# A four-layer convolution and attention kernel: another layout for the convolution results kept in device memory, and five images instead of four with a chunk convolved on VectorE

## The chip, the cores and the metric

The kernel runs on one core of one Trainium2 chip. The metric is the device time of one execution in microseconds (us), lower is better. The core has five engines that run side by side: TensorE (PE, matrix products into PSUM), VectorE (DVE), ScalarE (ACT), GpSimd (POOL) and SyncE (SP). SP and ACT also issue transfers (DMAs) between the device memory and the on-chip memory SBUF. Each engine works through its own queue in the order in which the program was laid out, and waits on semaphores where it needs another engine's result.

## The reference

The input x is 8 images of 384 channels and 32 x 32 pixels, in float32. Four residual layers follow each other, each on a group norm of x. Only the first matters here:

```python
def _dwproj(x, dw, g, b, pw):                     # for q, k and v
    y = depthwise_3x3(x, dw)                      # zero padding, one 3x3 filter per channel
    y = gelu(_bn(y, g, b))                        # batch norm over all 8 images and pixels
    return einsum('oc,bchw->bohw', pw, y)
q, k, v = _dwproj(gn(x), ...q), _dwproj(gn(x), ...k), _dwproj(gn(x), ...v)
attn = softmax(einsum('bhcn,bhcm->bhnm', q, k) * scale)      # 8 heads of 48 channels, 1024 pixels
x = x + _bn(w_out @ (attn applied to v), g_out, b_out)
```

The batch norm takes mean and variance over all images. So the three depthwise convolutions of all 8 images must be done, and their raw results kept somewhere, before the first GELU can run. The other three layers (a mixture of four small networks, a convolution with ternary weights, and an attention with sampled positions) are not touched by the change.

## The kernel before, in words

An image is held as 128 partitions x 3 chunks x 1024 pixels: channel 3p + c lies on partition p in chunk c.

**The convolution stage (first 390 us).** Each image b is group-normed by `norm(b)` in three steps. `begin` takes statistics on VectorE. `middle` (`gn_spread`) multiplies them with a small matrix on TensorE, into a PSUM bank of the pool `ps_mm`, and copies the result to `ga_a` (L118). `end` (`gn_scale`, then `affine`) does a second such product and writes the normed image into one of two padded buffers `pads`. Then the convolution runs in groups. A group g = 0 to 8 takes 42 channels (every third partition of chunk g // 3): `stack` copies them three times, shifted by a row, into a tile of 126 partitions (L318, three transfers on SP), and TensorE makes q, k and v of those 42 channels at once as 3 matmuls (one for each horizontal tap) for each half of the pixels, each of which leaves two records in the trace. The row 3 * i + v of the result `y` is channel i of q, k or v (v = 0, 1, 2). ScalarE copies each half from PSUM to `y` (L387), VectorE takes its statistics (L388), and ScalarE issues the stores to device memory (L394). Group `NGC` = 9 takes the two partitions left over in each of the three chunks (18 rows). `ps_mm` has four banks, so two groups' worth.

For the images in `ON_V` (0, 2, 4, 6) the groups 6, 7 and 8, chunk 2, are left out on TensorE. VectorE makes them itself, tap by tap (`convolve`: 9 instructions for each of q, k, v, L290 and L292, then `finish` with two statistics, one store and three small transfers that put the statistics where the groups would have put them). These steps wait in a list `taps`, and two of them are emitted after each group.

The order is written out by hand as a list `work` of (image, group). Before group n, the stacks of the groups up to nine ahead (`AHEAD`) are issued, and `begins` says at which n the norm of an image starts; its three steps follow at n, n + 1 and n + 2. At the end of the last image, `load_b(0)` loads the first image of the next stage, and `bn_moments` combines the statistics of a group over all images. The tile framework lays the program out for each engine: by this order, but an instruction whose inputs are ready in its own estimate may pass one that is not. It also inserts the waits, and transfers share a limited number of completion semaphores, so a transfer on SP can wait for an earlier one on ACT.

**The hand-over (390 to 405 us).** `bn_params` makes scale and shift (its power function runs on GpSimd, L97), L407 to L435 move them by small matmuls to the channel order, and the result is `ss0`. `values_tile` clears two tiles `vt` on GpSimd (L505). The weights of the next stage are loaded on SP (L512, L515), into memory that the convolution stage used.

**The attention stage (405 to about 1480 us).** For each image: `load_b` brings the raw q, k and v tiles in (three tiles of 512 KB for each of three chunks, from the pool `im` with five buffers), ScalarE applies scale, shift and GELU, TensorE projects, and runs the four head pairs of the attention. `gather_last` (into `ql`) and `place_last` (into `att`) are small transfers on SP between the parts. Loads of a coming image are issued when a buffer of `im` comes free.

A branch that is taken only if a softmax sum leaves a range (`redo`) holds the attention in a slower form, and reads `raw` too. It isn't taken in these runs.

Of the kernel before, what the change touches and what calls it, by code (L numbers as in the profile page):

```python
# [7 lines left out]
F32 = mybir.dt.float32  # L8
# [4 lines left out]
B, C, H, W = 8, 384, 32, 32  # L13
N = H * W
P = 128
KC = C // P
# [36 lines left out]
def tile_kernel(ctx: ExitStack, tc: tile.TileContext, i: dict, out: bass.AP):  # L53
    nc = tc.nc
# [148 lines left out]
    def image(name):  # L203
        return im.tile([P, KC, N], F32, tag="im", name=name)

    raw = [dram.tile([B, P, KC, N], F32, name=f"raw{v}") for v in range(3)]
    ss0 = const.tile([P, 3, 2, KC], F32, name="ss0")
    xmv = const.tile([P, B, KC, 2], F32, name="xmv")
    bn0 = bn_tiles(3 * GC, NGC + 1, "qkv")
    ON_V = (0, 2, 4, 6)  # L210
    acts = {}

    def load_b(b):
        acts[b] = {}
        for v in (0, 1, 2) if b == 0 else (2, 1, 0):
            acts[b][v] = image(f"g{v}_{b}")
            load_image(acts[b][v], raw[v][b])

    with ExitStack() as pa:
        wa = pa.enter_context(tc.tile_pool(name="a_w", bufs=1))  # L220
# [54 lines left out]
        def convolve(b, xn):  # L275

            state = {}

            def tap(v, t):
                dy, dx = t // 3 - 1, t % 3 - 1  # L280
                w = cwv[: 3 * GC, v, t : t + 1]
                if t == 4:
                    state["y"] = ya.tile([3 * GC, N], F32, tag="y", name=f"yv{b}_{v}")
                y = state["y"].rearrange("p (h w) -> p h w", h=H)
                r0, r1 = max(0, -dy), H - max(0, dy)
                c0, c1 = max(0, -dx), W - max(0, dx)
                d = y[:, r0:r1, c0:c1]
                f = xn[:, r0 + dy : r1 + dy, c0 + dx : c1 + dx]
                if t == 4:
                    nc.vector.tensor_scalar(d, f, w, None, ALU.mult)  # L290
                else:
                    nc.vector.scalar_tensor_tensor(d, f, w, d, ALU.mult, ALU.add)  # L292

            def finish(v):
                y = state["y"]
                for h in range(2):
                    nc.vector.bn_stats(vst[:, v, h, :], y[:, h * HALF : (h + 1) * HALF])
                nc.scalar.dma_start(out=raw[v][b, : 3 * GC, KC - 1, :], in_=y)
                for t in range(3):
                    nc.sync.dma_start(  # L300
                        out=cst[v : 3 * GC : 3, 3 * (KC - 1) + t, 2 * b : 2 * b + 2, :],
                        in_=vst[t : 3 * GC : 3, v, :, :],
                    )

            steps = []
            for v in range(3):
                steps += [lambda v=v, t=t: tap(v, t) for t in (4, 0, 1, 2, 3, 5, 6, 7, 8)]
                steps.append(lambda v=v: finish(v))
            return steps
# [30 lines left out]
        sts, taps, todo, later, normed = {}, [], {}, list(work), {0}  # L340

        def stacks(n):
            while later and len(work) - len(later) < n and later[0][0] in normed:
# [10 lines left out]
        for n, (b, g) in enumerate(work):  # L354
            if n in begins:
                b2 = begins[n]
                for k, f in enumerate(norm(b2)):
                    todo[n + k] = f, (b2 if k == 2 else 0)
                if b2 + 1 < B and b2 + 1 not in xts:
                    load_x(b2 + 1)  # L360
            if n in todo:
                f, b2 = todo.pop(n)
                f()
                normed.add(b2)
            stacks(n + AHEAD + 1)
            st = sts.pop((b, g))
            nch = GC if g < NGC else GR
# [5 lines left out]
            for h, k in steps:  # L373
# [11 lines left out]
                if k == 2:  # L385
                    hs = slice(h * HALF, (h + 1) * HALF)
                    nc.scalar.copy(y[:, hs], pk[h][: 3 * nch, :])  # L387
                    nc.vector.bn_stats(cst[: 3 * nch, g, 2 * b + h, :], y[:, hs])  # L388
            for v in range(3):
                if g < NGC:  # L390
                    to, of = raw[v][b, g % 3 : 3 * GC : 3, g // 3, :], y[v : 3 * GC : 3, :]
                else:
                    to, of = raw[v][b, 3 * GC :, :, :], y[v * GR : (v + 1) * GR, :]
                nc.scalar.dma_start(out=to, in_=of)  # L394
# [30 lines left out]
        for v in range(3):  # L425
# [66 lines left out]
    with ExitStack() as pb:  # L492
# [9 lines left out]

        def values_tile(s):
            t = wb.tile([P, NT8, 2 * NH0, 32], F32, name=f"vt{s}")
            nc.gpsimd.memset(t, 0.0)  # L505
            nc.gpsimd.memset(t[:, :, :, HQ0 : HQ0 + 1], 1.0)
            vts.append(t)

# [280 lines left out]
    with tc.If(redo > 0):  # L789
        with ExitStack() as pb:  # L790
# [13 lines left out]
            with tc.For_i(0, B) as bi:  # L804
                act = []
                for v in range(3):
                    g = work[v]
                    nc.sync.dma_start(
                        out=g, in_=raw[v][bass.ds(bi, 1)].rearrange("o p c n -> p (o c) n")
                    )  # L810
                    gelu_image(g, v)
                    act.append(g)
                for t in range(NT8):
# [1011 lines left out]
```

## Time and profile before

| What | us |
|---|---|
| median of 3 runs (lowest, highest) | 3829.66 (3827.58, 3834.88) |
| the profiled execution, its own time | 3834.06 |
| the span of that execution in the trace | 3832.2 |
| first convolution matmul, end of the last one | 21.68, 388.2 |
| first projection matmul of the attention stage | 404.93 |
| TensorE busy, of the span | 3646.2 (95%) |
| VectorE busy, of the span | 1823.4 (48%) |
| ScalarE busy, of the span | 1314.7 (34%) |

A line of a group view gives source line, engine, operation, the tile written <- the tiles read, shapes, count | busy us, mean ns of one | idle us just before, and what ended it. A line of a view in order of time begins with start and length in us; merged neighbours carry a count, and a bracket at the end gives the idle time ahead and what ended it. A line of the waits gives total us, number of times, longest. SPq and ACTq are the times that an engine spends issuing transfers.

### The profile page before, as it was taken

The numbers are of one execution on the slowest core, as the hardware profiler recorded it, in microseconds if no ns is written. First come the engines' busy times: TensorE is split into PE (matmuls) and PEld (weight loads), VectorE is DVE, ScalarE is ACT, GpSimd is POOL, SyncE is SP. The second block draws the span as 40 slices with busy tenths as digits, with TensorE's granted clock in tenths as the row PEclk, the third lists the DMA queues.
The fourth block names the chain that finished last, engine by engine and source line by source line (L and its number), as shares of the span: only waits on it lengthen the run. The fifth ranks groups of instructions, "written<-read, shape, count | busy, mean of one in ns | idle before, by whom it ended". The sixth has DMA issues, their size and how long they took to land.

```text
span 3832.2 us, 39353 instructions
## 1 busy us (share of the span) xinstructions
PE 3646.2 (95%) x15754; PEld 1520.9 (40%) x15754; DVE 1823.4 (48%) x2826; ACT 1314.7 (34%) x1557; POOL 235.5 (6%) x170
## 2 busy tenths in 40 slices
PE   7999899999999999999899999999999999999748
PEld 3444333333333333333344445444444444445213
DVE  5876223232323232332256665475656646565544
ACT  2222454554546353534112323223232222313102
POOL 0000000000000000000000100101011010100321
PEclk9999999999999999999899999999999999999868
DMA  6777211121202121111620000101001010010000
GB/s 200 245 235 241 100 53 43 53 61 40 74 24 72 27 69 38 59 49 50 233 81 33 17 33 19 48 17 33 33 17 34 17 50 17 25 42 1 17 17 18
DMA packets 83097, 242.64 MB, mean 63 GB/s; under 512 B 18336, under 2 KB 18864, under 8 KB 82520
## 3 DMA queue, kind: packets, MB, share of 16 engines
q1 hardware_dynamic: 69894, 200.56, 15.7%
q10 hardware_dynamic: 13008, 39.43, 3.0%
q8 instruction: 128, 2.10, 0.2%
q14 instruction: 67, 0.55, 0.0%
HBM read 122.78 MB, written 75.50 MB: 52 GB/s over the span
## 4 chain that ended last, share of the span: by engine, by line
PE 39%; DVE 9%; POOL 1%; issue 1%; ACT 1%; DVEq 0%; ACTq 0%; POOLq 0%
PE y L1251 10%; PE ph L1232 8%; DVE y L1320 5%; PE pq L1367 3%; PE pw L1341 3%; PE s L1504 3%; PE pf L1609 3%; PE pav L1520 2%; PE pss L1546 1%; DVE hd L1218 1%; DVE off L1415 1%; PE pk L1478 1%; PE xsb L1464 1%; PE pv L1487 1%; POOL tap L1323 1%
## 5 line engine op out<-in xcount | busy, mean ns | idle before, releaser
L630 ACT ACTIVATE p<-s 128x1024 f32<-128x1024 f32 x512 | 496.4, 1021 | 497.1 <-PE s L623 496.8
L1251 PE MATMUL y<-hd,w_sb 128*128 128x512 f32 x1080 | 493.4, 601 | 3.6 <-DVE hd L1218 3.6
L638 PE MATMUL pav<-p,vt 64*64 64x512 f32 x4096 | 486.4, 589 | 0.0
L1232 PE MATMUL ph<-h,w_sb 128*128 128x512 f32 x1104 | 483.6, 594 | 0.0
L623 PE MATMUL s<-qk,qk 48*64 48x512 f32 x3072 | 373.1, 600 | 4.4 <-ACT p L630 4.4
L381 PE MATMUL pk<-st,cw_sb 126*126 126x512 f32 x720 | 321.5, 608 | 3.6 <-DVE ga_a L118 3.3
L1232 PEld LDWEIGHTS ph<-h,w_sb 128*128 128x128 f32 x1104 | 207.8, 190 | 252.5 <-issue 249.4
L1251 PEld LDWEIGHTS y<-hd,w_sb 128*128 128x128 f32 x1080 | 198.8, 191 | 250.4 <-issue 236.3
L638 PEld LDWEIGHTS pav<-p,vt 64*64 64x64 f32 x4096 | 156.2, 133 | 285.3 <-issue 285.0
L595 DVE COPY ta<-pav 128x512 f32<-128x512 f32 x64 | 44.3, 692 | 439.1 <-PE pav L638 436.1
L1320 DVE SCALAR_TENSOR_TENSOR y<-h,tap,y 128x961 f32<-128x961 f32 (+1 forms) x184 | 233.5, 1295 | 1.6
L381 PEld LDWEIGHTS pk<-st,cw_sb 126*126 126x126 f32 x720 | 140.1, 197 | 177.7 <-issue 170.7
L1415 DVE SCALAR_TENSOR_TENSOR off<-q,dw_sb,off 128x225 f32<-128x225 f32 (+3 forms) x432 | 209.6, 542 | 1.9
L1240 ACT ACTIVATE hd<-ph,b_sb 128x512 f32<-128x512 f32 x180 | 122.6, 681 | 254.3 <-PE ph L1232 253.9
L623 PEld LDWEIGHTS s<-qk,qk 48*64 48x64 f32 x3072 | 102.6, 133 | 241.6 <-issue 184.7
L1341 PE MATMUL pw<-y,upw 128*128 128x512 f32 x288 | 128.6, 602 | 54.8 <-POOL y L1324 50.1
L78 DVE COPY qk<-pq 128x512 f32<-128x512 f32 x48 | 33.2, 692 | 293.1 <-PE pq L558 281.4
L387 ACT COPY y<-pk 126x512 f32<-126x512 f32 (+1 forms) x136 | 76.2, 583 | 254.4 <-DMA raw<-y 115.9
L1511 ACT ACTIVATE p<-s 128x1024 f32<-128x1024 f32 x96 | 93.0, 1021 | 171.8 <-PE s L1504 171.7
L146 ACT ACTIVATE h<-x,ss_d 128x1024 f32<-128x1024 f32 x42 | 49.6, 1231 | 287.6 <-DVE ss_d L132 287.6
L575 PE MATMUL po<-att,wo_sb 128*128 128x512 f32 x288 | 134.5, 617 | 9.5 <-DMA att<-al 9.5
L1218 DVE TENSOR_TENSOR hd<-hd,cb 128x512 f32<-128x512 f32 x180 | 122.9, 688 | 34.6 <-ACT hd L1240 34.2
(281 smaller groups left out, 4124.0 us busy)
## 6 DMA issues: line engine op xcount, KB each, us to landing
g<-raw SPq DMA_DIRECT2D x72, 512.0 KB
st<-pad SPq DMA_DIRECT2D x180, 168.0 KB
raw<-y ACTq DMA_DIRECT2D x180, 168.0 KB
xa<-in_x_dram SPq DMA_DIRECT2D x24, 512.0 KB
xh<-in_x_dram SPq DMA_DIRECT2D x48, 256.0 KB
f<-in_x_dram SPq DMA_DIRECT2D x24, 512.0 KB
f<-o SPq DMA_DIRECT2D x24, 512.0 KB
o<-ot SPq DMA_DIRECT2D x42, 256.0 KB
```

The costliest lines, as they stand in the source:

```text
L381: nc.tensor.matmul(pk[h].rearrange("p (h w) -> p h w", w=W)[: 3 * nch, :, o0 : o0 + c1 - c0], lhsT=lhs, rhs=rhs, start=(k == 0), stop=(k = ...
L575: nc.tensor.matmul(po, lhsT=wo0[:, c, m * P : (m + 1) * P], rhs=atts[b][:, c, hs], start=(c == 0), stop=(c == KC - 1),)
L623: nc.tensor.matmul(s[64 * k : 64 * k + 64, j * HALF : (j + 1) * HALF], lhsT=kt[r, k0 : k0 + 64], rhs=qt[r, h * HALF : (h + 1) * HALF], sta ...
L630: nc.scalar.activation(p, s, AF.Exp, scale=scale)
L638: nc.tensor.matmul(pav[k][64 * j : 64 * j + 64, :], lhsT=vts[b % 2][r, kc, 2 * hd : 2 * hd + 2, :].rearrange("p a b -> p (a b)"), rhs=p[r, ...
L1218: nc.vector.tensor_tensor(hd, hd, state["cb"], ALU.mult)
L1232: nc.tensor.matmul(ph, lhsT=w1[:, e, c, dc * P : (dc + 1) * P], rhs=state["h1"][c], start=(c == 0), stop=(c == KC - 1),)
L1240: nc.scalar.activation(hd, ph, AF.Relu, bias=b1[:, k : k + 1])
L1251: nc.tensor.matmul(y, lhsT=w2[:, e, dc, m * P : (m + 1) * P], rhs=state[h, k], start=(k == 0), stop=(k == NE * KC - 1),)
L1320: eng.scalar_tensor_tensor(d, f, tap2[:, c, t : t + 1], d, ALU.mult, ALU.add)
L1341: nc.tensor.matmul(pw[:, hs], lhsT=upw2[:, c, m * P : (m + 1) * P], rhs=y[:, c, hs], start=(c == 0), stop=(c == KC - 1),)
L1415: nc.vector.scalar_tensor_tensor(d, f, dw3[:, t : t + 1], d, ALU.mult, ALU.add)
```

## The change

The raw results are now one tensor in the form in which TensorE leaves them: `raw[image, group, 126 rows, pixels]`, and `raw_r` for the remainder group. A group's result is stored with one transfer instead of three. When an image is loaded, `load_raw` picks the rows of q, k or v out of it: three transfers of 42 rows for each chunk and one of two rows, where `load_image` used one of 128 rows. The branch `redo` loads in the same way.

`ON_V` becomes (0, 2, 3, 5, 6). After the groups two and three steps of `taps` are emitted in turn. The stores of the chunk made by VectorE are no longer issued in `finish` but by a new function `keep` four groups later: three strided stores and the three small statistics transfers, all on ScalarE's queue (the small ones were on SP).

The groups of an image come in the order 0, 1, NGC, 2, ... instead of NGC, 0, 1, .... A norm begins four groups earlier than the reach of the stacks instead of two, and its steps are two groups apart. In the last image `load_b(0)` comes at group 1 instead of 5, and the moments of groups 6, 7 and 8 are combined together after group 8. Last, the clearing of the first `vt` tiles on GpSimd is made to wait for the instruction that ends `ss0`.

```diff
-    raw = [dram.tile([B, P, KC, N], F32, name=f"raw{v}") for v in range(3)]
+    raw = dram.tile([B, NGC, 3 * GC, N], F32, name="raw")
+    raw_r = dram.tile([B, 3 * GR, N], F32, name="raw_r")
...
-    ON_V = (0, 2, 4, 6)
+    ON_V = (0, 2, 3, 5, 6)
     acts = {}
+
+    def load_raw(dst, b, v):
+
+        at = slice(b, b + 1) if isinstance(b, int) else b
+        for g in range(NGC):
+            nc.sync.dma_start(
+                out=dst[g % 3 : 3 * GC : 3, g // 3, :],
+                in_=raw[at, g, v : 3 * GC : 3, :].rearrange("o p n -> (o p) n"),
+            )
+            if g % 3 == 2:
+                nc.sync.dma_start(
+                    out=dst[3 * GC :, g // 3, :],
+                    in_=raw_r[at, v * GR + g // 3 : (v + 1) * GR : KC, :].rearrange(
+                        "o p n -> (o p) n"
+                    ),
+                )
...
-            load_image(acts[b][v], raw[v][b])
+            load_raw(acts[b][v], b, v)
...
-                nc.scalar.dma_start(out=raw[v][b, : 3 * GC, KC - 1, :], in_=y)
+                late.append((n_now[0] + 4, lambda: keep(v, y)))
+
+            def keep(v, y):
                 for t in range(3):
-                    nc.sync.dma_start(
+                    nc.scalar.dma_start(
+                        out=raw[b, 3 * (KC - 1) + t, v : 3 * GC : 3, :], in_=y[t : 3 * GC : 3, :]
+                    )
+                    nc.scalar.dma_start(
                         out=cst[v : 3 * GC : 3, 3 * (KC - 1) + t, 2 * b : 2 * b + 2, :],
                         in_=vst[t : 3 * GC : 3, v, :, :],
                     )
...
-        groups = [(NGC, *range(NGC - 3 if b in ON_V else NGC)) for b in range(B)]
+        groups = [[0, 1, NGC, *range(2, NGC - 3 if b in ON_V else NGC)] for b in range(B)]
...
-        begins = {max(2, work.index((b, NGC)) - AHEAD - 2): b for b in range(1, B)}
+        begins = {max(1, work.index((b, groups[b][0])) - AHEAD - 4): b for b in range(1, B)}
...
-                    todo[n + k] = f, (b2 if k == 2 else 0)
+                    todo.append((n + 2 * k, f, b2 if k == 2 else 0))
...
-            for v in range(3):
-                if g < NGC:
-                    to, of = raw[v][b, g % 3 : 3 * GC : 3, g // 3, :], y[v : 3 * GC : 3, :]
-                else:
-                    to, of = raw[v][b, 3 * GC :, :, :], y[v * GR : (v + 1) * GR, :]
-                nc.scalar.dma_start(out=to, in_=of)
-            for _ in range(2):
+            nc.scalar.dma_start(out=raw[b, g] if g < NGC else raw_r[b], in_=y)
+            for _ in range(2 + n % 2):
                 if taps:
                     taps.pop(0)()
+
+            while late and (late[0][0] <= n or n + 1 == len(work)):
+                late.pop(0)[1]()
             if b == B - 1:
-                if g == 5:
+                if g == 1:
                     load_b(0)
-                bn_moments(cst, g, bn0)
+
+                if g < NGC - 3 or g == NGC:
+                    bn_moments(cst, g, bn0)
+                elif g == NGC - 1:
+                    for k in range(NGC - 3, NGC):
+                        bn_moments(cst, k, bn0)
...
-        nc.vector.tensor_tensor(
+        scales = nc.vector.tensor_tensor(
             ss0.rearrange("p v s k -> p v (s k)"), ss0.rearrange("p v s k -> p v (s k)"),
...
-            nc.gpsimd.memset(t, 0.0)
+            zero = nc.gpsimd.memset(t, 0.0)
+
+            tc.add_manual_dep(
+                zero.ins, scales.ins.name, mybir.DependencyInfo(
+                    mybir.DependencyClass.Sync, mybir.DependencyReason.DATA
+                ), reason="scales first",
+            )
```

More of the change, by code (lines that the diff above doesn't have):

```diff
@@ L335, in tile_kernel @@
         AHEAD = 9
-        groups = [(NGC, *range(NGC - 3 if b in ON_V else NGC)) for b in range(B)]
+        groups = [[0, 1, NGC, *range(2, NGC - 3 if b in ON_V else NGC)] for b in range(B)]
         work = [(b, g) for b in range(B) for g in groups[b]]
-        begins = {max(2, work.index((b, NGC)) - AHEAD - 2): b for b in range(1, B)}
-        sts, taps, todo, later, normed = {}, [], {}, list(work), {0}
+        begins = {max(1, work.index((b, groups[b][0])) - AHEAD - 4): b for b in range(1, B)}
+        sts, taps, todo, later, normed, late, n_now = {}, [], [], list(work), {0}, [], [0]
         def stacks(n):
@@ L357, in tile_kernel @@
                 for k, f in enumerate(norm(b2)):
-                    todo[n + k] = f, (b2 if k == 2 else 0)
+                    todo.append((n + 2 * k, f, b2 if k == 2 else 0))
                 if b2 + 1 < B and b2 + 1 not in xts:
                     load_x(b2 + 1)
[L361 to L364, printed above, removed]
+            n_now[0] = n
+            for step in [t for t in todo if t[0] == n]:
+                todo.remove(step)
+                step[1]()
+                normed.add(step[2])
             stacks(n + AHEAD + 1)
@@ L807, in tile_kernel @@
                     g = work[v]
-                    nc.sync.dma_start(
-                        out=g, in_=raw[v][bass.ds(bi, 1)].rearrange("o p c n -> p (o c) n")
-                    )
+                    load_raw(g, bass.ds(bi, 1), v)
                     gelu_image(g, v)
```

## The prediction

> **What bounds the kernel now.** I read the page first (slices), then busy time by stretch, then each engine in order of time over the first 480 us, because the diff touches only the convolution stage, the hand-over, and the loads of the attention stage.
>
> ```profile
> PE   7999899999999999999899999999999999999748
> DVE  5876223232323232332256665475656646565544
> PEclk9999999999999999999899999999999999999868
> ```
>
> A slice is 95.8 us; the convolution stage is the first four. TensorE is nearly full in all of them while VectorE is at 5 to 8 tenths. The stretches (columns: length, then busy of PE, weight load, DVE, ACT, POOL, then granted clock, DMA share, GB/s):
>
> ```profile
> 20.00:390.00 370.00, 358.07 (x844) 151.35 (x844) 258.07 (x379) 100.05 (x156) 6.41 (x7) 0.95 0.70 231
> 390.00:405.00 15.00, 3.32 (x13) 3.07 (x13) 6.36 (x15) 3.23 (x4) 7.59 (x3) 0.59 0.87 321
> 405.00:1480.00 1075.00, 1070.62 (x7036) 397.03 (x7040) 310.52 (x511) 540.76 (x541) 1.82 (x3) 1.00 0.16 50
> ```
>
> So the stage is bound by TensorE (358 of 370 us), VectorE has 112 us free, then comes a hole of some 15 us, then an attention stage in which TensorE is 99.6% busy. TensorE in order of time:
>
> ```profile
> 21.68 8.08 PE L381 MATMUL pk<-st,cwr_sb 18*18 18x512 f32 x12 [9.97 <-DMA st<-pad]
> 29.69 12.69 PE L381 MATMUL pk<-st,cw_sb 126*126 126x512 f32 x24
> ...
> 123.50 2.70 PE L381 MATMUL pk<-st,cwr_sb 18*18 18x512 f32 x12
> 126.13 30.53 PE L381 MATMUL pk<-st,cw_sb 126*126 126x512 f32 x72
> ...
> 287.93 8.23 PE L381 MATMUL pk<-st,cw_sb 126*126 126x512 f32 x12 [3.06 <-DVE ga_a L118]
> ```
>
> A full group of 12 records costs 30.53/6 = 5.09 us, the remainder group (NGC) 2.70. The first two lines are slow: 8.08 instead of 2.70, and 12.69 instead of 10.18. The last line is the kernel's one bad meeting of norm and convolution: the next PSUM bank was held until VectorE copied ga_a, 3.06 us of stall, then 12 records at 8.23 instead of 5.09. VectorE's costs and the waits of the stage:
>
> ```profile
> L388 DVE BATCH_NORM_STATS2 cst<-y 126x6 f32<-126x512 f32 x120 | 79.0, 684 | 64.2 <-ACT y L387 64.1
> L292 DVE SCALAR_TENSOR_TENSOR yv<-xn,cwv_sb,yv 126x992 f32<-126x992 f32 x48 | 59.6, 1241 | 0.6
> L292 DVE SCALAR_TENSOR_TENSOR yv<-xn,cwv_sb,yv 126x961 f32<-126x961 f32 x48 | 58.1, 1211 | 0.9
> ```
> ```profile
> ACT y L387 <- DMA raw<-y: 113.5, 36, 7.8
> DVE cst L388 <- ACT y L387: 71.3, 34, 5.3
> ```
>
> ScalarE spends much of the stage issuing stores, and VectorE waits for its copies. What each transfer costs its queue (ns, min/median/max):
>
> ```profile
> L394 ACTq DMA_DIRECT2D raw<-y x204: 276/774/1872, 30.4 to 393.7; - x102
> L171 SPq DMA_DIRECT2D g<-raw x72: 327/430/902, 361.5 to 1453.1; - x72
> L298 ACTq DMA_DIRECT2D raw<-yv x12: 332/338/1066, 42.5 to 348.7; - x12
> ```
>
> A transfer of every third partition costs 774 ns to issue, an unstrided one 338. And the hand-over and the attention stage's SP queue:
>
> ```profile
> 395.98 3.16 DVE L407 COPY both<-bnsc_qkv 126x10 f32<-126x10 f32 x1
> 399.20 0.17 DVE L408 COPY both<-bnsh_qkv 126x10 f32<-126x10 f32 x1
> ```
> ```profile
> 395.61 3.51 POOL L505 MEMSET vt<- 128x4096 f32 x1
> ```
> ```profile
> 507.13 59.15 SPq L171 DMA_DIRECT2D g<-raw  x5
> 588.44 8.07 SPq L471 DMA_DIRECT2D att<-al  x12
> ```
>
> [...] the same small copy takes 0.17 us, but 3.16 while the memset runs. [...] full groups run at half pace from 29.69 to about 34.5, although narrow matmuls had run since 21.68[...]. [...]
>
> **Part by part.**
>
> *Five images on VectorE instead of four* (3 and 5 in, 4 out). Three full groups go: 3 x 5.09 = **-15.3 us** of TensorE. VectorE gains 27 taps (3 x 0.72 + 12 x 1.241 + 12 x 1.211 = 31.6), 6 statistics (4.1) and one copy (0.7), and loses 6 statistics (4.1): +32 us, about 29 with the overlap of successive instructions. So it goes from 258 to some 288.
>
> *2.5 taps per group.* 150 steps run out at group 60 of 65. Those groups take TensorE 52 x 5.09 + 8 x 2.70 = 286 us at full pace; now the stage takes 1.10 times that (388.2 - 21.7 - 7.9 at the start = 358.6 against 60 x 5.09 + 8 x 2.70 = 327), so 314. VectorE needs some 281 (288 less the last five groups' work). That leaves 33 us, and another 17 can be caught up in the last five groups, where it has no taps. Its waits for other things than ScalarE were 13.2 (images), 9.6 (xn), and 6.3 + 6.2 + 3.0 (norm chain) = 38 us in this stage. So it just fits. I charge **+5 us** for banks held a little longer (bounds -2, when the wider spacing of the norm steps removes the 287.93 stall, and +45, when VectorE is late at many norms).
>
> *Group order 0, 1, NGC, and norms begun 4 ahead, two groups apart.* Groups 0 and 1 read only chunk 0 of the first image. Their three transfers issue from 14.03 (about 0.85 each) and land near 18.5, against 21.68 for the first matmul now: -3. [...] now 8.08 - 2.70 + 12.69 - 10.18 = 7.9 are lost. Together up to -9; I take **-7** (bounds -9 and 0, if the weights are not there or later stacks fall behind).
>
> *One store per group.* ScalarE: 3 x 0.77 becomes 0.34, so some 120 us of issue time go. The convolved chunk's stores become three strided ones and its three small statistics transfers move from SP to ScalarE: 15 x 6 x 0.77 = 69 us, in bursts of 4.6 us, four groups late. A burst delays the next copies by up to 4 us; two groups' worth of PSUM (10 us) hides that, and without it each of 15 bursts would cost its 4 us. Small waits of TensorE for y (7.8 us in all) shrink: **-2** (bounds -6 and +3).
>
> *Hand-over.* The memset waits for the scales, so the locked copy's **-3.0** is certain if its order holds; the two memsets (2 x 3.5 us) then lie in VectorE's 9 us of idleness after the scales. The last copy, at 391.48 behind a store that issued slowly, should come near the last matmul's end: -2.5. Three moments at the end instead of one: +1.1. Image 0's loads, 27 x 0.77 + 9 x 0.4 = 24 us of SP instead of 4, begin eight groups before the end: hidden. But the two loads of image 1 (24 transfers, 17 us) may stand ahead of the weights as six do now (at 380.59, weights at 394.47): +3, bounds 0 and +10. Sum **-1.5**.
>
> *Attention stage.* SP gets 36 transfers per image instead of 9, +20 us of its 177. The last of them start when the values' matmuls free their buffer (566 us in image 0). Twelve take 9 us, and the att transfers stand at 588.44: 22 us of cover. Queued behind are att and ql, for which the output projection (635) and the last pair's scores wait. **+1**, bounds 0 and +15.
>
> Sum: -15.3 + 5 - 7 - 2 - 1.5 + 1 = **-19.8**; I round to -18, as stage sums seldom arrive whole. Against the profiled span 3832.2 that is 3814; the profiled execution (3834.06) lay 4.4 us above the median of 3829.66, so for the median **3812**.
>
> **Rivals.**
> (1) *VectorE is the new bound and eats most of it.* For: 281 + 38 us of 314. Against: taps fill its waits, and a late VectorE no longer waits for ScalarE (71 us now). Gain 4 to 11: 3819 to 3826.
> (2) *Slower: PSUM banks held at the norms.* Each norm puts two small results into the convolution's four banks, freed only by a VectorE copy in its queue. Behind taps of 1.2 us the 287.93 episode repeats; it cost 3.06 + 8.23 - 5.09 = 6.2 us, and happened at one of 14 such places. From about six more places on (37 us against a gain of some 25 without the +5) it is slower by over 0.2%; at eight, 3855. For: VectorE is busy for 281 of 314 us, its waits not counted. Against: the chain's steps are now two groups apart.
> (3) *The saving is absorbed*: the order that is built isn't the one written, SP's loads reach TensorE in each image (3 us x 7), or the weights come 10 us late: within 7.7 us of now.
>
> **How the numbers follow.** A measurement here can tell about 0.2%, 7.7 us. The sum as worked out (gain 12 to 26): 0.52, own range 3804 to 3818. Rival 1: 0.20, of which three quarters are still over 0.2%. Rival 3: 0.08. Rival 2: 0.16, a quarter of that within 0.2%. A gain above 26: 0.04. Faster 0.52 + 0.15 + 0.04 = 0.71; same 0.05 + 0.08 + 0.04 = 0.17; slower 0.12. The range 3800 to 3836 leaves out about 0.16.
>
> **What would show it.** Right: first full group before 20 us and full pace by 24; last convolution matmul near 366; VectorE's wait for y well under 71 us; the L407 copy at 0.17 us; TensorE over 99% in the attention stage. Wrong: more stalls before L381 put down to ga_a or ve_a; the weights issued over 10 us after the last matmul; att or ql landing behind g<-raw; a longer hole.

## The result, and the profile after

The changed kernel takes **3852.52 us** (median of 4 runs, 3849.47 to 3855.56), against 3832.27 for the kernel before on the same chip: a ratio of 1.0054, with a 95% interval of 1.0036 to 1.0071. It is slower by half a per cent, 40 us from the forecast of 3812 and outside its range. The profiled execution has a span of 3847.7 us (before 3832.2).

Where the 15.5 us of span came from, between three points that can be read in TensorE's order of time:

| | before | forecast | after |
|---|---|---|---|
| first convolution matmul | 21.68 | 18.7 | 21.82 |
| end of the last one | 388.2 | 368.9 | 394.1 |
| first projection matmul | 404.93 | 384.1 | 422.09 |
| from there to the end | 3427.3 | 3428.3 | 3425.6 |

(The forecast's column adds its terms to the column before: -15.3 + 5 - 7 - 2 for the convolutions, -1.5 for the hand-over, +1 for the rest.) So the convolutions ended 25.2 us later than forecast, the hand-over took 12.8 us more (28.0 instead of 15.2), and the rest took 2.7 us less. The slices of the page for after, then its stretches (columns as before):

```profile
PE   6889799999999999999799999999999999999747
DVE  7787123232323232323346566475656636565554
PEclk9899899999999999999899999999999999999868
```
```profile
20.00:390.00 370.00, 335.07 (x799) 142.07 (x800) 286.57 (x405) 97.84 (x149) 7.29 (x7) 0.93 0.64 210
390.00:405.00 15.00, 7.32 (x22) 4.50 (x20) 4.72 (x17) 4.08 (x5) 3.52 (x2) 0.77 0.59 186
405.00:1480.00 1075.00, 1053.52 (x6923) 390.34 (x6924) 305.23 (x503) 534.09 (x533) 5.87 (x4) 0.99 0.20 57
```

In the first stretch TensorE is now idle for 35 us instead of 12, VectorE is at 286.6 (forecast 288), and the DMA engines move less, 210 GB/s for 231, at a share of 0.64: neither VectorE nor the DMA engines are full. The third stretch has lost 17 us of TensorE, all at its beginning, as will be seen. TensorE in order of time, the first two lines and the long stalls:

```profile
21.82 12.42 PE L406 MATMUL pk<-st,cw_sb 126*126 126x512 f32 x24 [10.03 <-DMA st<-pad]
34.18 2.71 PE L406 MATMUL pk<-st,cwr_sb 18*18 18x512 f32 x12
...
61.23 0.56 PE L116 MATMUL gna_a<-mv_a,g_sb 128*128 128x2 f32 x2 [8.57 <-DVE xmv L143]
142.53 0.56 PE L116 MATMUL gna_a<-mv_a,g_sb 128*128 128x2 f32 x2 [5.86 <-DVE mv_a L110]
188.84 17.58 PE L406 MATMUL pk<-st,cw_sb 126*126 126x512 f32 x36 [8.33 <-DMA cst<-vst]
...
283.21 0.56 PE L116 MATMUL gna_a<-mv_a,g_sb 128*128 128x2 f32 x2 [6.95 <-DVE xmv L143]
```

The slow start did shrink, from 7.9 us lost to 12.42 - 10.18 = 2.2. Before the change the 18-row matmul records took 1.01 to 1.06 us each, and the 126-row ones after them 1.03 to 1.22 until 34.0; now the 126-row ones take 0.95 to 1.19 until 26.1, and 0.58 to 0.59 after that. The granted clock reads 1.00 over these matmuls in both, so it is the half pace alone that is shown, and that "half clock" stands for in the expectations. The waits inside the convolutions, however, add up to 33.1 us, against 8.4 before. With them the end can be summed up again: 388.2, less 15.3 for the three groups and 5.6 for the slow start, plus 24.7 of added waits, is 392.0, and 394.1 was measured. None of the waits is the wait that was feared: no bank is held at ga_a or ve_a. TensorE stands before a norm's first small product because the statistics are late, or before a stack that hasn't come. ScalarE and VectorE, on the other hand, have time (waits from 20 to 390 or 400 us, and VectorE's groups):

```profile
ACT y L412 <- DMA raw<-y: 12.1, 3, 4.9
```
```profile
DVE cst L413 <- ACT y L412: 63.7, 43, 6.3
```
```profile
L413 DVE BATCH_NORM_STATS2 cst<-y 126x6 f32<-126x512 f32 x114 | 77.7, 688 | 65.4 <-ACT y L412 64.9
L310 DVE SCALAR_TENSOR_TENSOR yv<-xn,cwv_sb,yv 126x992 f32<-126x992 f32 x60 | 74.5, 1241 | 0.9
L310 DVE SCALAR_TENSOR_TENSOR yv<-xn,cwv_sb,yv 126x961 f32<-126x961 f32 x60 | 72.2, 1204 | 0.5
```

ScalarE's idle time ahead of its copies that ended with a store's landing fell from 113.5 us to 12.1, and the transfers themselves got cheaper to issue or fewer (ns, min/median/max):

```profile
L219 SPq DMA_DIRECT2D g<-raw x216: 743/753/1678, 379.6 to 1477.6; - x108
L414 ACTq DMA_DIRECT2D raw<-y x57: 327/333/1155, 29.9 to 394.7; - x57
L320 ACTq DMA_DIRECT2D raw<-yv x45: 774/822/899, 39.5 to 371.4; - x45
```

The waiting has moved to SP, whose queue carries the stacks and the image loads. Its longest waits from 100 to 350 us (total us, times, longest), in the kernel before and after:

```profile
SPq L318 <- DMA raw<-y: 19.6, 24, 4.8
...
SPq L327 <- DMA raw<-y: 7.5, 10, 2.6
```
```profile
SPq L341 <- DMA raw<-y: 43.9, 14, 7.7
SPq L350 <- DMA raw<-y: 21.2, 6, 7.7
SPq L341 <- DMA raw<-yv: 16.8, 6, 4.7
```

All of SP's waits for ScalarE's transfers (stores and moments) in that stretch come to 41 us in 46 waits before, and 108 us in 41 waits after. Each is three times as long. The hand-over, on VectorE and on SP, and ahead of them the weights in the kernel before:

```profile
394.47 0.33 SPq L512 DMA_DIRECT2D wq_sb<-in_wq_dram  x1
```
```profile
398.63 0.16 DVE L435 COPY both<-bnsc_qkv 126x10 f32<-126x10 f32 x1
```
```profile
379.56 3.18 SPq L219 DMA_DIRECT2D g<-raw  x3
...
415.02 0.42 SPq L224 DMA_DIRECT2D g<-raw_r  x1
415.49 0.36 SPq L83 DMA_DIRECT2D gbo_sb<-in_gbo_dram  x1
...
417.84 0.37 SPq L546 DMA_DIRECT2D wq_sb<-in_wq_dram  x1
```
```profile
422.09 7.04 PE L592 MATMUL pq<-g,wq_sb 128*128 128x512 f32 x12 [19.58 <-DMA g<-raw]
```

The copy that took 3.16 us beside the memset (the forecast's "locked" one: 395.98 to 399.15, the memset 395.61 to 399.12) takes 0.16 without it. That a memset always does this is not shown: beside the second one before the change (from 402.83) VectorE's next lines took 0.34 (three instructions), 0.21 and 0.17 us, as they do with none now. But the sorting loads hold SP from 379.6 to 415.4, and the weights, which were issued at 394.47 before, follow at 417.84. The scales were ready at 403.3, and TensorE waited 19.6 us.

### The profile page after: what moved, and what is told of

Its sections match the earlier page's. It is cut to its first block, busy times and chain, and to the rows that moved or that the text cites. A ratio compares the mean times of both kernels' runs of the same rounds, so it can differ in the third digit from the quotient of the medians.

```text
span 3847.7 us, 39573 instructions
## 1 busy us (share of the span) xinstructions
PE 3626.8 (94%) x15718; PEld 1511.4 (39%) x15718; DVE 1850.3 (48%) x2854; ACT 1313.6 (34%) x1551; POOL 236.2 (6%) x170
## 4 chain that ended last, share of the span: by engine, by line
PE 39%; DVE 8%; POOL 1%; issue 1%; ACT 1%; DVEq 0%; ACTq 0%; POOLq 0%
PE y L1283 10%; PE ph L1264 8%; DVE y L1352 5%; PE pq L1399 3%; PE s L1536 3%; PE pw L1373 3%; PE pf L1641 3%; PE pav L1552 2%; PE pss L1578 1%; DVE hd L1250 1%; DVE off L1447 1%; PE pk L1510 1%; PE xsb L1496 1%; PE pv L1519 1%; POOL tap L1355 1%
## 5 line engine op out<-in xcount | busy, mean ns | idle before, releaser
L406 PE MATMUL pk<-st,cw_sb 126*126 126x496 f32 (+1 forms) x684 | 308.5, 612 | 20.0 <-DMA st<-pad 11.7
L592 PE MATMUL pq<-g,wq_sb 128*128 128x512 f32 x288 | 131.6, 607 | 19.6 <-DMA g<-raw 19.6
L310 DVE SCALAR_TENSOR_TENSOR yv<-xn,cwv_sb,yv 126x961 f32<-126x961 f32 (+1 forms) x120 | 146.7, 1223 | 1.4
```

The source lines that it names most:

```text
L406: nc.tensor.matmul(pk[h].rearrange("p (h w) -> p h w", w=W)[: 3 * nch, :, o0 : o0 + c1 - c0], lhsT=lhs, rhs=rhs, start=(k == 0), stop=(k = ...
L592: nc.tensor.matmul(pq, lhsT=w_in[v][:, c, pr * P : (pr + 1) * P], rhs=acts[b][v][:, c, h * HALF : (h + 1) * HALF], start=(c == 0), stop=(c ...
```

## Experiments

There are two theories. *Transfers*: SP is late, because it waits for ScalarE's transfers, and the weights are late behind SP's sorting loads. *VectorE*: its added work (28.5 us more in the first stretch) makes the statistics late (the forecast's rivals 1 and 2). In the traces of the kernels before and after, the transfers of SP and of ScalarE signal their completion on the same eight semaphores (numbers 101 to 107 and 109), given out over both queues. There are 1125 pairs of successive transfers with one semaphore before and 1235 after, 298 and 198 of them from one queue to the other, and in every pair the earlier one had landed before the issue of the later one ended. So a stack on SP can wait for a store of ScalarE that came a few places before it, though neither needs the other's data.

**e1: the weights on ScalarE's queue.** In the changed kernel:

```diff
-            nc.sync.dma_start(out=t, in_=i[nm])       # wq, wk, wv; wo likewise
+            nc.scalar.dma_start(out=t, in_=i[nm])
```

> Only the four weight loads of the attention stage move from SP's queue to ScalarE's, so that they no longer stand behind the 36 loads of image 0. If the hole before the first projection (19.58 us of wait after the small matmuls) is the weights' place in SP's queue, TensorE begins to project some 15 to 17 us earlier, as soon as q's three chunks have their GELU (near 406 us of the span), and the kernel comes out at about 3836 us, no different from before within 0.2%. If the loads of image 0 themselves are what is late (SP ends its stacks at 379.5), the gain is 5 us or less and the wait is then put down to the loads.

Measured: 3838.9 us, ratio 1.0022 (1.0012 to 1.0033). The hole closes, and the stalls in the convolutions stay (32.8 us):

```profile
402.99 7.54 PE L592 MATMUL pq<-g,wq_sb 128*128 128x512 f32 x12 [2.16 <-ACT g L511]
```

So some 12 of the 20 us of loss (ratio 1.0022 instead of 1.0054) are the weights' place in SP's queue. The first scores come 13.1 us earlier (423.07 instead of 436.14), less than the first projection, as GELU still waits for the sorting loads.

**e2 and e3: less work on VectorE.** e2 puts `ON_V` back to (0, 2, 4, 6). e3 leaves out three of the nine taps on VectorE, so its output is another function's; it is read for the time alone.

> The changed kernel with images 0, 2, 4, 6 on VectorE, as before the change; everything else stays. Three full groups come back, +15.3 us of TensorE. If VectorE's load is the cause of the 33 us of stalls in the convolution stage, they fall to under 10 and the last convolution matmul ends near 386 (394 in the changed kernel); the time falls by about 8 us to 3844. If the stalls come from the new layout and the transfers, they stay and the time rises by 15 us to about 3867.

> Five images, but three of the nine taps of each convolution on VectorE are left out (so the convolved chunk is not the reference's); the steps keep their places. VectorE loses 5 x 9 x 1.2 = 54 us of work, TensorE and all transfers keep theirs. If VectorE is the bound, TensorE's stalls at the norms and at the stacks go, the last convolution matmul ends near 365 to 370, and the time falls by 25 us or more to 3827 or less. If it is the place of the transfers by itself, less than 10 us.

e2: 3863.4 us, ratio 1.0075 (1.0058 to 1.0092), stalls of 31.9 us, the last matmul at 410.8, 16.7 later, of which the three groups that came back to TensorE are 15.3. e3: 3851.1, ratio 1.0050 (1.0034 to 1.0065), stalls of 32.0 with VectorE at 238 us instead of 287. Taking work off VectorE gave nothing back, so in the changed kernel its load is not what makes the stalls.

**e4: the late stores really late.** In the built program the stores of `keep` stood up to five groups earlier than written, since a ready instruction may pass others. e4 ties each to the copies of the group for which it was written.

> In the built order of the changed kernel the convolved chunk's stores stand on ScalarE's queue up to five groups ahead of where they are written (that of image 2's last third at group 22, written at 27). Here an ordering edge puts each of them behind the copies of the group where it is written, really four groups behind. If ScalarE stopping in front of those stores until VectorE has finished is the cause (through it the copies, and through the semaphores that transfers share, SP's stacks), the wait of SP for stores falls from some 130 us to half, the stalls from 33 to about 12, and the time falls by 15 to 25 us to about 3832. If VectorE's own lateness at the norms is the cause, it stays within 5 us of the changed kernel.

3850.7 us, ratio 1.0044 (1.0027 to 1.0061), stalls of 29.0 us. Their place isn't the cause either.

**e5 to e8: the parts alone, on the kernel before.** e5 is the layout: stacked `raw`, one store per group, the sorting loads, the chunk of VectorE in three strided stores. e6 is the group order and the norms' timing. e7 is the five images and the pace. e8 is the group order with the memset behind the scales.

```diff
e5 -                for v in range(3): ... nc.scalar.dma_start(out=to, in_=of)
e5 +            nc.scalar.dma_start(out=raw[b, g] if g < NGC else raw_r[b], in_=y)
e6 +  groups = [[0, 1, NGC, *range(2, ...)] ...];  begins ... - AHEAD - 4;  todo[n + 2 * k] = ...
e7 +  ON_V = (0, 2, 3, 5, 6);  for _ in range(2 + n % 2):
e8 +  groups as in e6;  the dependence of the memset on `scales`
```

> The kernel before with the layout alone: stacked raw, one store per group, the sorting loads, VectorE's chunk stored by three strided transfers where one stood; four images on VectorE, the group order, the norms and the small transfers on SP as before. Theory L (the single 504 KB store per group holds SP's stacks through the shared semaphores): TensorE's stalls of 5 to 9 us appear here too, the last convolution matmul ends 15 to 25 us later than 388, and with the weights behind 36 loads on SP (about +15) the time is 3855 to 3875. Theory N (the norms' earlier place and the group order cause the stalls): the convolutions end at 385 to 389, and only the weights cost: 3840 to 3850.

> The kernel before with the group order (two full groups, the remainder, the rest) and the norms' new timing (two groups earlier, steps two groups apart) alone. Theory N: stalls of 5 to 9 us on gna or on stacks at several images, the last convolution matmul 10 to 25 us later than with the half clock saved (382.5), so 393 to 407, and the time 3838 to 3855. Theory L: none of them, the half clock's 5.6 us saved, 3822 to 3828.

> The kernel before with five images (0, 2, 3, 5, 6) on VectorE at two and three steps in turn alone, VectorE's store where it finishes as before. If the saving of three groups (15.3 us) comes through with the old layout and norms: the last convolution matmul at 373 to 380 and 3817 to 3825. If VectorE's load or its banks stand against it: 3827 to 3840.

> The kernel before with the group order alone (norms as near as before) and the zeroing of the values tile held behind the scales. Both theories: half clock -5.6 and the locked copy -3 (hand-over 11.35 to 8.3), so 3822 to 3825; if the order alone already makes the norms or the stacks late, 3828 to 3840.

| | median | ratio (interval) | last convolution matmul | stalls before it | first projection |
|---|---|---|---|---|---|
| before | 3831.7 | | 388.2 | 8.4 | 404.93 |
| e5 layout | 3880.6 | 1.0123 (1.0106 to 1.0140) | 421.2 | 36.1 | 449.54 |
| e6 order, norms | 3832.9 | 1.0003 (0.9994 to 1.0012) | 391.1 | 21.2 | 406.25 |
| e7 five images | 3829.0 | 0.9990 (0.9984 to 0.9997) | 381.8 | 19.1 | 401.36 |
| e8 order, scales | 3834.6 | 1.0003 (0.9995 to 1.0012) | 389.6 | 21.1 | 404.41 |

The layout alone costs 49 us: it is the whole loss and more. SP in e5, and what TensorE waits for just after:

```profile
179.56 7.49 SPq L319 DMA_DIRECT2D cst<-vst  x3
187.15 13.58 SPq L337 DMA_DIRECT2D st<-pad  x9
200.77 4.46 SPq L171 DMA_DIRECT2D xa<-in_x_dram  x3
```
```profile
214.79 0.56 PE L116 MATMUL gna_a<-mv_a,g_sb 128*128 128x2 f32 x2 [6.99 <-DVE mv_a L110]
```

Three tiny transfers take SP 7.5 us (from 100 to 350 us such three took 2.3 to 4.4 before the change, and 2.3 to 12.6 in e5) and nine stacks 13.6, 1.5 us each, where issuing one takes 0.75 (before the change the fastest took 745 ns, the median 757). The image load behind them starts at 200.77, its statistics begin at 208.95, and TensorE, for which the product that needs them comes next in the program, stands still. So 12 us of waits in SP's queue are 7 us of TensorE some 14 us later. e6 and e8 show that order and norms bring nothing: what the start saves (5.6 us) comes back as stalls, 21 us instead of 8. e7 brings 6.4 of the 15.3 us to the convolutions' end.

**e9 to e12: the store in three.** e9: the changed kernel with each group's store as three transfers of 42 neighbouring rows to the same place. e10: the same with every third row. e11: e5 with e9's edit. e12: e9 with e1's edit.

```diff
-            nc.scalar.dma_start(out=raw[b, g] if g < NGC else raw_r[b], in_=y)
+            for v in range(3):                                   # g < NGC
+                at = slice(v * GC, (v + 1) * GC)                 # e10: slice(v, 3 * GC, 3)
+                nc.scalar.dma_start(out=raw[b, g, at, :], in_=y[at, :])
```

> The changed kernel with each full group's store issued as three transfers of 42 neighbouring rows (168 KB each) to the same place in the stacked raw, instead of one of 504 KB. Theory S (a 504 KB store takes about three times as long to land as a 168 KB one, and SP's next transfers wait for it: between 100 and 350 us SP waited 37 us for stores before, 98 after): SP's waits for stores fall to 35 to 55 us, TensorE's stalls of 5 to 9 us mostly go, the last convolution matmul ends at 366 to 382 instead of 394, and with the weights still 17 us late 3822 to 3840. Rival (the loads, the placement in DRAM or the image norms, not the store's size): SP's waits and the stalls stay, 3845 to 3858.

> The same, with the three transfers taking every third row, as the kernel before issues them (0.77 us each on ACT's queue instead of 0.33). Theory S: as e9_thirds within 5 us, 3822 to 3842. If what matters is that slow issues on ACT pace it behind SP, and not the size, only this one gets better and e9_thirds does not.

> The layout alone (e5_layout) with the group's store in three transfers of 42 neighbouring rows. Theory S: of its 33 us in the convolutions most comes back, the last convolution matmul at 386 to 400 instead of 421, the hole before the first projection stays (15 to 19), 3843 to 3860 instead of 3881. Rival: 3872 to 3888.

> e9_thirds with the four weight loads on ACT's queue. Theory S: e9_thirds less 13 to 18 us, 3806 to 3824, under both kernels. Rival: as e1_weights_act, 3832 to 3842.

| | median | ratio (interval) | last conv. matmul | SP's waits, 100 to 350 | ScalarE's waits there | TensorE waits for ScalarE's copies |
|---|---|---|---|---|---|---|
| after | 3852.5 | 1.0054 (1.0036 to 1.0071) | 394.1 | 108 | 33 | under 1.5 |
| e9 | 3851.2 | 1.0050 (1.0032 to 1.0068) | 404.2 | 31 | 97 | 25.3 |
| e10 | 3842.6 | 1.0031 (1.0021 to 1.0041) | 400.0 | 54 | 110 | 21.9 |
| e12 | 3850.0 | 1.0045 (1.0027 to 1.0062) | 405.2 | 38 | 106 | 25.5 |
| e5 | 3880.6 | 1.0123 (1.0106 to 1.0140) | 421.2 | 86 | 10 | under 1.5 |
| e11 | 3839.5 | 1.0019 (1.0012 to 1.0026) | 396.5 | 9 | 130 | 8.0 |

(SP's and ScalarE's waits: for stores and moments, in us; ScalarE's are idle time of the engine, with the transfers that it issues meanwhile.) On the layout alone the edit gives back 41 of 49 us: 24.7 in the convolutions, and most of the rest in the hand-over, as SP is no longer late with the sorting loads and the weights (from the last convolution matmul to the first projection 13.5 us instead of 28.3). In e9 and e10 too the weights come in time: the first projection follows the small matmuls after 2.16 us. So e12, which was expected to gain 13 to 18 us over e9 by e1's edit, gains nothing. On the changed kernel the edit does to SP's waits what was expected, but the convolutions end 10 us *later*, not 12 to 28 earlier. The waiting has gone to ScalarE:

```profile
SPq L337 <- DMA raw<-y: 3.5, 4, 1.0
```
```profile
ACT y L406 <- DMA raw<-y: 111.9, 30, 8.0
```

(The longest such waits in e11: SP's from 100 to 350 us, ScalarE's from 20 to 400.) There ScalarE can bear it. In e9 it can't; ScalarE in order of time, then TensorE:

```profile
212.99 0.82 ACTq L320 DMA_DIRECT2D raw<-yv  x1
214.90 2.17 ACTq L417 DMA_DIRECT2D raw<-y  x3
217.56 0.80 ACTq L323 DMA_DIRECT2D cst<-vst  x1
218.40 0.94 ACTq L320 DMA_DIRECT2D raw<-yv  x1
220.69 0.77 ACTq L323 DMA_DIRECT2D cst<-vst  x1
221.94 0.79 ACTq L320 DMA_DIRECT2D raw<-yv  x1
223.11 0.77 ACTq L323 DMA_DIRECT2D cst<-vst  x1
223.93 3.50 ACT L146 ACTIVATE pad<-xa,ss_a 128x1024 f32<-128x1024 f32 x3 [11.91 <-DMA st<-pad]
227.34 1.51 ACT L412 COPY y<-pk 126x512 f32<-126x512 f32 x3
```
```profile
227.95 4.43 PE L406 MATMUL pk<-st,cw_sb 126*126 126x512 f32 x6 [8.92 <-ACT y L412]
```

The six transfers of one output of VectorE's chunk, and a group's three between them, keep ScalarE from 213.0 to 223.9, though they are 7.1 us of issue: the other 3.8 us are gaps between them, and the view ends ScalarE's idle time with the landing of a transfer (st<-pad). The next image's normalisation, and behind it the PSUM copies, wait until 223.9 and 227.3, and TensorE stands still for 8.9 us until a copy has freed a bank. So the waits in this queue stop the engine and not only the transfers: ScalarE computes nothing for 11.9 us while it issues them.

**e13, e14, e16: who fills ScalarE's queue.** e13 is e9 with the moments' transfers back on SP. e16 is e9 with all six transfers of an output on GpSimd's queue. e14 is e11 with five images, so it has no new norms or order.

```diff
 # e13: the second line only, with nc.sync; e16: both
-                    nc.scalar.dma_start(out=raw[b, 3 * (KC - 1) + t, ...], in_=y[t : 3 * GC : 3, :])
-                    nc.scalar.dma_start(out=cst[v : 3 * GC : 3, ...], in_=vst[t : 3 * GC : 3, v, :, :])
+                    nc.gpsimd.dma_start(...)                     # both, same arguments
```

> e9_thirds with the moments of VectorE's chunk (three 2 KB transfers to cst for each of its outputs) back on SP's queue, the three stores of the chunk still on ACT's. Theory K (what remains in e9_thirds is ACT's queue: six transfers for each output of the chunk, each waiting for a transfer before it, stand ahead of the PSUM copies and of the next image's normalisation): TensorE's waits for ACT's copies fall from 35 us to under 18, the last convolution matmul from 404 to 380 to 392, 3828 to 3840. Rival (the norms' earlier place makes them): unchanged within 5 us, 3845 to 3856.

> e11_layout_thirds with five images on VectorE at two and three steps in turn; order, norms and moments on SP as in the kernel before. If norms and order have no share in the stalls: the three groups' 15.3 us come, less the 3 to 9 us that e7_five lost beside them: 3824 to 3834. If VectorE's added load costs here: 3836 to 3845.

> e9_thirds with all six transfers of each output of VectorE's chunk on GpSimd's queue. Theory K: TensorE's waits for ACT's copies fall under 18 us as in e13 or further, 3815 to 3838. Rival: 3845 to 3856; and if transfers from GpSimd's queue are slow or hold VectorE, over 3856.

e13: 3840.1 us, ratio 1.0020 (1.0013 to 1.0027); the last matmul at 390.1 instead of 404.2, TensorE's waits for ScalarE's copies 12.9 instead of 25.3. e14: 3849.5, ratio 1.0045 (1.0029 to 1.0060); with the old norms and order it waits 24.5 us for the copies, where four images (e11) waited 8.0, and the time is above both forecasts. So it is not the norms or the order; that it is the chunk's transfers on ScalarE, e16 shows. In this layout the fifth image costs 9 us of convolution time instead of saving 15. e16: 3833.1, ratio 1.0001 (0.9993 to 1.0010), and the convolutions end at **376.3**, 11.9 us before the kernel before:

```profile
40.77 0.76 POOL L320 DMA_DIRECT2D raw<-yv  x1 [28.16 <-DVE ga_a L118]
42.45 0.53 POOL L323 DMA_DIRECT2D cst<-vst  x1 [0.93 <-DVE dm_a L121]
42.97 0.51 POOL L320 DMA_DIRECT2D raw<-yv  x1
```
```profile
381.54 0.59 PE L449 MATMUL pmove<-both,sel_sb 126*128 126x20 f32 x2 [5.21 <-DVE both L441]
403.85 7.09 PE L597 MATMUL pq<-g,wq_sb 128*128 128x512 f32 x12 [19.07 <-DMA g<-raw]
```

TensorE no longer waits for ScalarE's copies. None of SP's and of ScalarE's waits from 100 to 350 us is for the chunk's transfers any more (43.2 and 20.7 us in the changed kernel). GpSimd has little else to do in this stage (busy for 8.2 of 350 us in e9), and it issues such a transfer in 0.51 us where ScalarE takes 0.77 to 0.82. What was gained is then lost to the weights again: 19.1 us.

**e15, e17, e18: versions under both kernels.** e17 is e16 with e1's edit. e15 is built on the kernel before, with its layout and norms: five images, the memset behind the scales, the remainder group third in the first image only, and the stores of the last two groups issued after ScalarE's last copy. e18 is e15 with the store and the moments of VectorE's chunk on GpSimd's queue.

> On the kernel before, without the layout, the norms and the late stores: five images on VectorE, the zeroing of the values tile behind the scales, two full groups ahead of the remainder group in the first image alone, and the stores of the last two groups issued after ACT's last copy. From e7_five (3829): scales -3, half clock -5, last copy -4: 3813 to 3822, under both kernels. If the saved microseconds turn into waits for the norms instead: 3822 to 3832.

> e16_thirds_pool with the four weight loads on ACT's queue (e1's edit). The hole of 19 us before the first projection closes to 2 to 4: 3814 to 3822, and the end of the convolutions (376) and the hand-over (5.2) that the prediction summed up are there with the three queues' loads apart. If the convolutions' end moves back with the changed order of transfers: 3824 to 3836.

> e15_best with the four transfers of each output of VectorE's chunk (its one store and the three of its moments) on GpSimd's queue. If the waits for gna in e15_best (17 us) come from SP's queue being late by these transfers: 3814 to 3823. If they come from the image loads' own place behind the stacks: 3823 to 3830.

| | median | ratio (interval) | last convolution matmul | first projection |
|---|---|---|---|---|
| e15 | 3826.9 | 0.9988 (0.9980 to 0.9996) | 387.7 | 399.78 |
| e17 | 3822.3 | 0.9973 (0.9964 to 0.9983) | 375.6 | 386.24 |
| e18 | **3815.2** | 0.9954 (0.9942 to 0.9967) | 375.3 | 387.86 |

```profile
386.24 6.96 PE L597 MATMUL pq<-g,wq_sb 128*128 128x512 f32 x12 [2.16 <-ACT g L516]
...
402.68 1.56 PE L570 MATMUL pv<-wv_sb,g 128*128 128x384 f32 x4 [1.27 <-ACT g L516]
```

In e17 the first projection comes 18.7 us earlier than in the kernel before (404.93), close to the 20.8 that the forecast summed up, but the total gains 10: the first scores come 13.2 us earlier (406.62 for 419.81), as GELU waits for the sorting loads, those of the third tile last. Another 3 us are at the very end (from the start of the last matmul of ph to the end of the span 316.5 us, before 313.7; 316.6 in e16), which no edit touches; that is not explained. e18 doesn't have the sorting loads. It is the fastest kernel here, 17 us under the kernel before: the chunk's transfers on GpSimd's queue alone bring 12 us (e15 to e18).

## Why the prediction was wrong

- **One store per group, -2 (bounds -6 and +3): the step that failed first.** It counted ScalarE's issue time, which fell as said, and took the rest of the stage to be unchanged. The layout alone moves the end of the convolutions by +33.0 (e5), and storing each group in three transfers gives 24.7 of that back (e11). The step priced what a transfer costs the queue that issues it. It put at nothing what it costs the other queue that waits for its semaphore: SP's waits for ScalarE's transfers rose from 41 to 108 us. That queues can wait so was known and stands in the description of the kernel; and of the 113.5 us in 36 times that the prediction read as issuing stores, three issues of 0.77 us each would fill only some 83, an estimate; the rest was waiting for one to land.
- **"two groups' worth of PSUM (10 us) hides that": failed.** The bursts of six transfers were taken to be 4.6 us of issue. In e9 the one shown, with its waits and a group's three stores between, lasted 10.9 and met the next norm. TensorE's waits for ScalarE's copies were 25.3 us in e9, 12.9 in e13 (half of the transfers gone from ScalarE) and under 1.5 in e16 (all). In the changed kernel itself this stayed hidden, as SP was the later of the two.
- **The hand-over, -1.5: one term mis-sized.** The copy beside the memset (3.16 us before, 0.16 after; -3.0 in the sum) and the earlier last copy came as said: from the last matmul to the scales' product 5.2 us instead of 11.35. The weights behind the sorting loads were put at +3 with a bound of +10; they cost 17.4 (404.93 - 399.52 = 5.4 before, 22.8 after). The estimate took image 0's loads as hidden, and put image 1's ahead of the weights. It was image 0's own 36 transfers that stood there: they began only at 379.6, SP being late, and held SP for 36 us, where 24 were counted. In e16, where the convolutions end early, TensorE waits 19.1 us all the same.
- **Five images, -15.3: right in the groups, not in the end.** A full group takes 35.54/7 = 5.08 us in e16. With VectorE's own transfers out of the way the end does move, by 11.9 (e16) and 12.9 us (e18). In e16 20.0 us of stalls stay, 16.1 of them before a norm's first product; at the one of 269.5 the loads of the image were issued only at 255.0, and VectorE waited for them three times.
- **VectorE held banks, +5: wrong cause.** In the changed kernel no stall is put down to ga_a or ve_a (5.0 us in e9, 4.6 in e13), and taking a third of the taps away changed nothing (e3). For that kernel rivals 1 and 2 fall with it; what VectorE's load would cost where SP is not late, e3 does not test. Rival 3, "the saving is absorbed", named both real mechanisms, loads on SP reaching TensorE and late weights, but with 3 us an image and 10 us, and was given 0.08.
- **Group order, -7: half.** What the slow start loses shrank by 5.6, to 2.2; the 2.0 left of it in the bound of -9 was the author's estimate. The early start did not come: the first group's three stacks were issued by 16.6, but the last had landed only at 21.82, where 18.5 was counted. And in all kernels that begin so, TensorE stalls at about 59 to 67 us for 2.8 to 9.7 us, in all but e8 as the statistics of the next image but one come late: in the changed kernel SP begins to load that image only at 48.05.
- **Attention stage, +1: right**, but for its sign: -1.7 for all that follows the first projection, with 36 transfers per image and TensorE busy for 1050.6 of the 1055 us from 425 to 1480. The cover argued for held, with the att transfers at their old distance from the projection:

```profile
606.42 8.08 SPq L499 DMA_DIRECT2D att<-al  x12
```

What stays open: whether it is the size of the single store or the smaller number of transfers between two stacks that makes SP's waits long, as e9 to e11 change both. One such wait lasts 2.6 us on average in the changed kernel and 2.9 in e5, and 0.9 to 1.3 in e9, e10, e11 and e16. Against the size alone speaks what the packets of ScalarE's queue show, if they are counted off in the order of issue: a whole store has landed after a median of 3.9 us (4.5 in e5), one of three after 3.9 as well (e9, e11; by the completions on the semaphores 4.1 after the end of the issue in the changed kernel, and 3.6 for the thirds of the kernel before), and not in a third of the time, which e9's expectation supposed. Then SP would come to the semaphore sooner after the store's issue; that is not shown. Open, too, are the 3 us at the end of e17. The changed kernel with GpSimd's queue but whole stores was not run.

## What to carry to other kernels

In these runs a transfer cost its own queue the issue time (0.33 us for a whole store, 0.77 for every third row), and the queue that shares completion semaphores with it waits until it landed (86 us of SP's time from 100 to 350 us in e5, and 9 in e11). Before merging or moving transfers, list SP's waits by what they wait for, and look at what stands behind each on its engine. Keep bursts of small transfers off the engine that evacuates PSUM where such waits stand (TensorE waited 25.3 us for ScalarE's copies in e9, under 1.5 in e16): a nearly idle queue, for whose transfers SP and ScalarE were not seen to wait, here GpSimd's, gave 12 us for an edit of two words (e15 to e18). When loads are multiplied, follow the last transfer of the queue (here the next stage's weights), not only the loads themselves.

## What the runs showed that was not expected

The sum of the two queues' waits for stores and moments from 100 to 350 us does not go with the time: 149 us before, 142 after, 127 in e9, 139 in e11, and 96 in e5, the slowest. Nor does SP's share alone: in e16, e17 and e18, where the convolutions end earliest, SP waits 69 to 77 us for stores, more than in the kernel before (41), but in 51 to 58 short waits. As the runs read, what counts is which queue waits, how long at a time, and what stands behind. GpSimd's queue issued a transfer of 42 strided partitions in 0.51 us, faster than ScalarE (0.77 to 0.82) or SP (0.75). And after 8 us of 18-row matmuls at the start the full groups still ran at half pace from 29.7 to 34.0 us (1.03 to 1.22 us a record for 0.58), while full rows from the start lost only 2.2 us.
